# Layer 0's products in four 64x64 array tiles, with sums that stay in PSUM for a whole image

## The chip, the cores and the metric

The kernel runs on one core of one Trainium2 chip. The metric is the device time of one execution in microseconds (us). Five engines work side by side[...]: TensorE (PE in the profile, with PEld for its weight loads), VectorE (DVE), ScalarE (ACT), GpSimd (POOL) and SyncE (SP), which here only issues transfers. TensorE writes its results to PSUM, which has eight banks of 512 float32 values per partition; ScalarE and VectorE take them out from there.

## The reference, cut to what matters

Four layers follow each other on an input of 4 images with 64 x 64 = 4096 positions and 64 channels, all in float32. Layer 0 is the one that is changed:

```
q, k, v = x Wq + bq,  x Wk + bk,  x Wv + bv        # 4 images, 4096 x 64 each
attn    = softmax over keys of (q k^T)             # 4096 x 4096 per image
out[n]  = sum over queries m of attn[m, n] * v[m]  # summed over the queries, not over the keys
x       = gamma * out + x
```

Layer 1 is a block with two pointwise convolutions, a 3x3 depthwise convolution, a channel gate and two more pointwise convolutions. Layer 2 is an attention of the image with itself, and layer 3 an attention with 32 channels, followed by a normalisation over all images.

The unusual point of layer 0 is that `out` is summed over the queries. A query's row of `attn` can only be scaled once its whole sum of exponentials is known. That scale (one over the sum) goes into `v`, which gives a scaled row per query named `vq`. Then `out` is the product of `vq` with the plain exponentials, added up over all 4096 queries.

## The kernel before, in words

`fast_path` does the work; `general_path` is a second version that runs only if a check of the sums at the end of `fast_path` fails.

**Layout.** `X` holds image b as 128 partitions x 2048 columns: partitions 0 to 63 are the 64 channels of the first half of the positions, partitions 64 to 127 those of the second half. PSUM is split by two pools: `pp` has three tiles of two banks each (`new_ps`), and `pa` has two tiles of one bank each (`new_acc`).

**Layer 0, one tile of 128 queries** (`scores(t)`, t from 0 to 31). For each of four column groups g, four matmuls (line L1045) fill one `ps` tile of 128 queries x 1024 keys. Each works on 64 of the array's rows (64 channels) and 64 of its columns (64 queries), so that four of them together fill the array; I call four such matmuls a quad. A float32 matmul is two MATMUL records in the profile. ScalarE then takes the exponential of the whole `ps` tile into a tile `e` in SBUF (line L1050), and adds up its row sums on the way. `scale(t)` on VectorE turns the sums into `vq` (L1059, L1061, L1062).

**The products** (`products(p, half)`, L1070) take a pair of query tiles. Here the 128 queries are the contraction, so each matmul uses all 128 array rows and 64 columns, and two of them (one for each half of the keys) fill the array. A call runs two query tiles x two column groups x two key halves, that is 8 matmuls or four such pairs, into two `acc` banks. After each call VectorE adds the two banks, times gamma, into a running sum `m.y` in SBUF (`stt`, L1077).

**Order.** ScalarE, VectorE and TensorE run in the order in which the program is written. `run()` steps through a list `items`, one for every tile of queries; after each item the functions that fall due at it are called. For layer 0 an item is all four score quads of a tile in a row, and then comes one call of `products` (four pairs). Two generators fill in other work, the lanes `conv` and `misc`: `conv` runs layer 1 of the image before (`layer1`), `misc` loads, the projections of the next image (`project0`) and other preparations. A lane is ticked twice an item with the item's nominal cost (3.6), and makes a step when its own nominal time has come. The lanes take their PSUM from `new_ps` as the scores do.

**Layer 2**, which serves for comparison below, is built alike: `scores(n)` (L1259) are four quads of 64x64 and `products(n)` (L1276) are four quads of 64x64 too, since there the two query halves go to separate accumulators.

**Padding.** `layer1` takes a new padded buffer `pad` for each of its two halves and has GpSimd write its zero border (L1145 to L1147) each time.

Of the kernel before, what the change touches and what calls it, by code (L numbers as in the profile page):

```python
# [8 lines left out]
F32 = mybir.dt.float32  # L9
# [682 lines left out]
def fast_path(ctx: ExitStack, tc: tile.TileContext, a: dict, out: bass.AP, bad):  # L692
# [10 lines left out]
    tp = ctx.enter_context(tc.tile_pool(name="tp", bufs=2))  # L703
    xn = ctx.enter_context(tc.tile_pool(name="xn", bufs=1))
    sm = ctx.enter_context(tc.tile_pool(name="sm", bufs=2))
    pp = ctx.enter_context(tc.tile_pool(name="pp", bufs=3, space=PSUM))
    pa = ctx.enter_context(tc.tile_pool(name="pa", bufs=2, space=PSUM))

    PW = 65

    def new_ps(name="ps"):
        return pp.tile([128, 1024], F32, tag="ps", name=name)

    def new_acc(name="acc"):
        return pa.tile([128, 512], F32, tag="acc", name=name)

    def new_e(name="e"):
        return ep.tile([128, 2048], F32, tag="e", name=name)
# [4 lines left out]
    def new_big(name):  # L723
        return big.tile([128, 4096], F32, tag="big", name=name)
# [254 lines left out]

    def project0(b):  # L980
        x, m = X[:, b], im[b]
        m.q, yv = new_big("q"), new_big("yv")
        m.y = yv[:, 0:2048]
        m.v = yv[:, 2048:4096].rearrange("p (t c) -> p t c", c=C)
        once = ((0, "once"), (0, "v"), (1, "once"), (1, "v"))
        for j, w in once if b else ((0, "q"), (0, "v"), (1, "q"), (2, "q"), (1, "v"), (3, "q")):
            ps = new_ps()
            if w == "once":
                for o in range(2):
                    for s in range(2):  # L990
                        mm(
                            ps[64 * o : 64 * o + 64, bass.ts(s, 512)], wq[64 * s : 64 * s + 64, 0:64],
                            tok(x, s, 2 * j + o), start=True, stop=True,
                        )
                qs = m.q.rearrange("p (s n) -> p s n", s=2)
                for o in range(2):
                    own, other = slice(64 * o, 64 * o + 64), slice(64 - 64 * o, 128 - 64 * o)
                    n = bass.ts(2 * j + o, 512)
                    act(  # L999
                        qs[own, :, n], ps[own, :].rearrange("p (s n) -> p s n", s=2),  # L1000
                        AF.Identity, bias=bqk[own, :],
                    )
                    nc.sync.dma_start(out=qs[other, :, n], in_=qs[own, :, n])
            elif w == "q":
                for o in range(0, 128, 64):
                    for s in range(2):
                        mm(
                            ps[o : o + 64, bass.ts(s, 512)], wq[64 * s : 64 * s + 64, o : o + 64],
                            tok(x, s, j), start=True, stop=True,
                        )  # L1010
                for s in range(2):
                    nc.vector.tensor_scalar_add(
                        m.q[:, 2048 * s + 512 * j : 2048 * s + 512 * j + 512], ps[:, bass.ts(s, 512)], bqk
                    )
            else:
                for i in range(8):
                    mm(ps[:, bass.ts(i, 128)], x[:, bass.ts(8 * j + i, 128)], wv, start=True, stop=True)  # L1017
                for s in range(2):
                    nc.vector.tensor_add(
                        m.v[:, 16 * s + 8 * j : 16 * s + 8 * j + 8, :],  # L1020
                        ps.rearrange("p (t s c) -> p t s c", s=2, c=C)[:, :, s, :],
                        bv.unsqueeze(1).to_broadcast([128, 8, C]),
                    )
            yield 3.4

    between = []

    def layer0(b):  # L1030
        x, m, first = X[:, b], im[b], len(items)
        tiles = {}

        def scores(t):
            es = [new_e() for _ in range(2)]
            zs = sm.tile([128, 4], F32, tag="zs", name="zs", bufs=4)
            vq = sm.tile([128, C], F32, tag="vq", name="vq", bufs=4)
            for g in range(4):
                if g == 2 and between:
                    between.pop()()  # L1040
                ps = new_ps()
                for c in range(2):
                    for r in range(2):
                        rows_ = slice(64 * r, 64 * r + 64)
                        mm(  # L1045
                            ps[64 * c : 64 * c + 64, bass.ts(r, 512)],
                            m.q[rows_, 128 * t + 64 * c : 128 * t + 64 * c + 64],
                            x[rows_, bass.ts(g, 512)], start=True, stop=True,
                        )
                act(  # L1050
                    es[g // 2][:, bass.ts(g % 2, 1024)], ps, AF.Exp, bias=SHIFT0,
                    accum_out=zs[:, g : g + 1],
                )
            tiles[t] = es, vq, zs

        def scale(t):
            es, vq, zs = tiles[t]
            tot = sums0[:, b, t : t + 1]
            nc.vector.tensor_reduce(tot, zs, AX.X, ALU.add)  # L1059
            rec = sm.tile([128, 1], F32, tag="rec", name="rec")  # L1060
            nc.vector.reciprocal(rec, tot)  # L1061
            nc.vector.tensor_scalar_mul(vq, m.v[:, t, :], rec)  # L1062

        def products(p, half):
            accs = [new_acc() for _ in range(2)]
            for t in (2 * p, 2 * p + 1):
                es, vq, _ = tiles[t]
                for g in range(2):
                    for r in range(2):
                        mm(  # L1070
                            accs[g][64 * r : 64 * r + 64, :], vq,
                            es[half][:, 1024 * g + 512 * r : 1024 * g + 512 * r + 512],
                            start=t == 2 * p, stop=t == 2 * p + 1,
                        )
            for g in range(2):
                cols = bass.ts(2 * half + g, 512)
                stt(  # L1077
                    (x if p == 15 else m.y)[:, cols], accs[g], gam0,
                    (m.y if p else x)[:, cols], ALU.mult, ALU.add,
                )  # L1080

        for t in range(32):
            items.append((lambda t=t: scores(t), 3.6))
        for p in range(16):
            for half in range(2):
                at(first + 2 * p + 2 + half, lambda p=p, half=half: products(p, half))
        for t in range(32):
            at(first + t, lambda t=t: scale(t))


    def norm(x, y):
# [29 lines left out]
        for jp in range(2):  # L1121
            cols = bass.ts(jp, 1024)
            nc.vector.tensor_mul(y[:, cols], y[:, cols], x[:, cols])
            yield 1.8

    def layer1(b):
        x = X[:, b]

# [12 lines left out]
        yw = yg.rearrange("c (s q p h) -> c p q s h", s=2, p=2, h=H)  # L1141
        ysum = sm.tile([128, 8], F32, tag="ysum", name="ysum")
        for r in (1, 0):
            pad = new_pad()
            nc.gpsimd.memset(pad[:, 0:PW], 0.0)  # L1145
            nc.gpsimd.memset(pad[:, 65 * PW : 66 * PW + 2], 0.0)
            nc.gpsimd.memset(  # L1147
                pad[:, PW : 65 * PW].rearrange("p (w h) -> p w h", h=PW)[:, :, 0:1], 0.0
            )
            inner = pad[:, PW + 1 : 65 * PW + 1].rearrange("c (p q s h) -> c q p s h", p=2, s=2, h=PW)  # L1150
            for j in range(4):
                ps = new_ps()
# [92 lines left out]
    def layer2(b):  # L1245
# [7 lines left out]
        def scores(n):  # L1253
            ib = n // 8
            for jb in range(4 * (n % 8), 4 * (n % 8) + 4):
                ps = new_ps()
                for r, c in quads:
                    rows_ = slice(64 * r, 64 * r + 64)
                    mm(  # L1259
                        ps[64 * c : 64 * c + 64, bass.ts(r, 512)],  # L1260
                        m.ko[rows_, 128 * jb + 64 * c : 128 * jb + 64 * c + 64],
                        m.ko[rows_, bass.ts(2 * ib + r, 512)], start=True, stop=True,
                    )
                if jb % 2 == 0:
                    e = new_e()
                es[n, jb] = e[:, bass.ts(jb % 2, 1024)]
                act(es[n, jb], ps, AF.Exp, bias=SHIFT2, accum_out=m.zs[:, jb, ib : ib + 1])  # L1267

        def products(n):
            ib = n // 8  # L1270
# [94 lines left out]
    def layer3(b):  # L1365
# [23 lines left out]
        def products(n):  # L1389
# [3 lines left out]
                st["y"] = new_acc()  # L1393
            if mc % 10 == 9 or (last and n >= 60):
                if mc == 9:
                    st["z"] = new_acc("accz")
                for k in range(4):
                    mm(  # L1398
                        st["z"][32 * k : 32 * k + 32, :], ones[:, 0:32], e[:, bass.ts(k, 512)],
# [166 lines left out]

    def begin_out(i):
        b, g = i // 2, i % 2
        ps = new_ps("out")
        for k in range(8):  # L1570
            mm(
                ps[:, bass.ts(k, 128)], X[:, b, 1024 * g + 128 * k : 1024 * g + 128 * k + 128], ident,
                start=k % 4 == 0, stop=False,
            )
        return ps
# [125 lines left out]
        nc.vector.tensor_reduce(cnt, acc[0:1, 0:4], AX.X, ALU.add)  # L1701
        nc.vector.tensor_scalar(bad, cnt, -1.0, float(total), ALU.mult, ALU.add)

    with tc.manual_schedule(engines={mybir.EngineType.PE, mybir.EngineType.Activation, mybir.EngineType.DVE}):
        run()
        finish()

# [47 lines left out]
```

## Time and profile before

| | |
|---|---|
| time, median of 3 runs | 2637.28 us (2636.89 to 2637.54) |
| span of the profiled execution | 2635.8 us |
| TensorE busy | 2607.8 us, 99% |
| ScalarE busy | 1730.5 us, 66% |
| VectorE busy | 1331.1 us, 51% |
| GpSimd busy | 17.1 us, 1% |
| layer 0 (with the lanes' work in it) | about 17 to 1029 us of the span |

A busy TensorE is not a TensorE at its peak: matmuls overlap, their ends are modelled, and a wait inside the array counts as busy. The start of a group of matmuls in the timeline is exact, and so is the distance from one group's start to the next; that distance, and not the busy time, is what a group costs. PEld rows show when weights are loaded: in an undisturbed stream a weight load is done during the matmuls before it.

### The profile page before, as it was taken

The page shows a single profiled execution, that of the slowest core. Times are in us where ns is not written, and L with a number is a line of the kernel's source. Part 1 is how long each engine was busy: PE and PEld are TensorE (multiplying, and loading weights), DVE is VectorE, ACT ScalarE, POOL GpSimd, SP SyncE. Part 2 cuts the span into 40 slices and gives each one's busy share as a digit, 9 for nine tenths or more (in the row PEclk, how much of TensorE's full clock was granted, in tenths as well). Part 3 has the DMA queues.
Part 4 walks back from the last instruction along what each step waited for, and adds up shares of the span by engine and source line. Part 5 has one row for each costly group of instructions (what it writes and reads, how often), then busy time and mean ns, then how long its engine had stood idle before and what let it go on. Part 6 is the DMA issues. An engine that isn't in the chain of part 4 may idle for free.

```text
span 2635.8 us, 50835 instructions
## 1 busy us (share of the span) xinstructions
PE 2607.8 (99%) x22429; PEld 821.6 (31%) x22429; DVE 1331.1 (51%) x1542; ACT 1730.5 (66%) x2814; POOL 17.1 (1%) x67
## 2 busy tenths in 40 slices
PE   8999999999999999999999999999999999999998
PEld 3333233333323323333333322233322233322223
DVE  3232397633876338721772148800068600098997
ACT  4555656656565665666656678855678755578886
POOL 2000000000000000000000000000000000000000
PEclk9999999999999999999999999999999999999999
DMA  3000000001000100010010000010000010010002
GB/s 74 1 17 1 17 14 5 1 17 33 1 1 1 33 17 1 1 33 17 1 33 17 17 1 1 2 33 1 17 1 2 1 33 1 1 33 2 1 2 66
DMA packets 24538, 36.46 MB, mean 14 GB/s; under 512 B 3724, under 2 KB 12149, under 8 KB 24309
## 3 DMA queue, kind: packets, MB, share of 16 engines
q1 hardware_dynamic: 23285, 32.03, 5.5%
q8 instruction: 178, 2.92, 0.5%
q0 software_dynamic: 704, 0.56, 0.1%
q10 hardware_dynamic: 320, 0.54, 0.1%
q14 instruction: 51, 0.42, 0.1%
HBM read 4.80 MB, written 4.19 MB: 3 GB/s over the span
## 4 chain that ended last, share of the span: by engine, by line
PE 97%; ACT 1%; DVE 1%; issue 0%; DMA 0%; SPq 0%; ACTq 0%
PE acc L1070 17%; PE ps L1045 17%; PE acc L1276 17%; PE ps L1259 16%; PE ps L1377 11%; PE acc L1412 10%; PE ps L1132 2%; PE accz L1398 1%; PE ps L1017 1%; PE ps L1223 1%; PE ps L1200 1%; PE ps L1102 1%; PE ps L1356 1%; PE ps L931 0%; ACT e L1267 0%; PE ps L1289 0%
## 5 line engine op out<-in xcount | busy, mean ns | idle before, releaser
L1050 ACT ACTIVATE e<-ps 128x1024 f32<-128x1024 f32 x512 | 517.0, 1025 | 310.9 <-PE ps L1045 211.4
L1267 ACT ACTIVATE e<-ps 128x1024 f32<-128x1024 f32 x512 | 517.1, 1025 | 302.3 <-PE ps L1259 302.2
L1405 DVE TENSOR_TENSOR tg<-tg,e 128x2048 f32<-128x2048 f32 x213 | 488.1, 2292 | 24.0 <-ACT e L1383 5.7
L1045 PE MATMUL ps<-X,q 64*64 64x512 f32 x4096 | 474.5, 598 | 6.2 <-ACT q L999 1.7
L1259 PE MATMUL ps<-ko 64*64 64x512 f32 x4096 | 467.2, 591 | 2.2 <-ACT ko L1241 1.6
L1070 PE MATMUL acc<-e,vq 128*64 128x512 f32 x2048 | 467.4, 598 | 0.0
L1276 PE MATMUL acc<-e,X 64*64 64x512 f32 x4096 | 464.7, 591 | 0.3 <-DVE X L1077 0.3
L1077 DVE SCALAR_TENSOR_TENSOR yv<-acc,gam,yv 128x512 f32<-128x512 f32 x224 | 167.9, 750 | 324.8 <-PE acc L1070 314.0
L1382 ACT ACTIVATE e<-ps 128x1024 f32<-128x1024 f32 x256 | 262.8, 1027 | 84.4 <-PE ps L1377 70.3
L1171 DVE SCALAR_TENSOR_TENSOR y<-pad,vec,y 128x1024 f32<-128x1024 f32 x240 | 308.1, 1284 | 8.1 <-ACT pad L1155 1.0
L1377 PE MATMUL ps<-tg,ph 32*64 32x512 f32 x4096 | 311.0, 613 | 0.5 <-ACT e L1382 0.3
L1412 PE MATMUL acc<-e,tg 128*32 128x512 f32 x2048 | 271.8, 603 | 0.0
L1383 ACT ACTIVATE e<-ps 128x1024 f32<-128x1024 f32 x256 | 261.4, 1021 | 0.0
L1259 PEld LDWEIGHTS ps<-ko 64*64 64x64 f32 x4096 | 153.6, 132 | 292.0 <-issue 199.9
L1045 PEld LDWEIGHTS ps<-X,q 64*64 64x64 f32 x4096 | 143.0, 132 | 320.0 <-issue 222.1
L1276 PEld LDWEIGHTS acc<-e,X 64*64 64x64 f32 x4096 | 155.2, 133 | 277.1 <-issue 272.3
L1070 PEld LDWEIGHTS acc<-e,vq 128*64 128x64 f32 x2048 | 136.1, 136 | 314.6 <-issue 293.4
L1284 DVE TENSOR_TENSOR ph<-ph,acc 128x512 f32<-128x512 f32 x16 | 11.0, 688 | 392.2 <-ACT ph L1283 392.2
L1377 PEld LDWEIGHTS ps<-tg,ph 32*64 32x64 f32 x4096 | 80.5, 129 | 217.2 <-issue 119.7
L1267 ACT ACTIVATION_READ_ACCUMULATOR e<-ps 128x1 f32 x512 | 106.5, 208 | 0.0
L1412 PEld LDWEIGHTS acc<-e,tg 128*32 128x32 f32 x2048 | 43.6, 108 | 201.0 <-issue 196.9
L1050 ACT ACTIVATION_READ_ACCUMULATOR e<-ps 128x1 f32 x512 | 106.0, 207 | 0.0
(195 smaller groups left out, 981.5 us busy)
## 6 DMA issues: line engine op xcount, KB each, us to landing
xn<-t SPq DMA_DIRECT2D x64, 128.0 KB
ph<-tg SPq DMA_DIRECT2D x64, 128.0 KB
ko<-ko SPq DMA_DIRECT2D x16, 256.0 KB
xr<-in_x_dram SPq DMA_DIRECT2D x13, 256.0 KB
q<-q SPq DMA_DIRECT2D x12, 256.0 KB
out_dram<-o SPq DMA_DIRECT2D x8, 256.0 KB
out_dram<-o SPq DMA_DIRECT2D x4, 512.0 KB
xr<-in_x_dram ACTq DMA_DIRECT2D x2, 128.0 KB
```

What stands on the lines that cost most here:

```text
L1045: mm(ps[64 * c : 64 * c + 64, bass.ts(r, 512)], m.q[rows_, 128 * t + 64 * c : 128 * t + 64 * c + 64], x[rows_, bass.ts(g, 512)], start=Tru ...
L1050: act(es[g // 2][:, bass.ts(g % 2, 1024)], ps, AF.Exp, bias=SHIFT0, accum_out=zs[:, g : g + 1],)
L1070: mm(accs[g][64 * r : 64 * r + 64, :], vq, es[half][:, 1024 * g + 512 * r : 1024 * g + 512 * r + 512], start=t == 2 * p, stop=t == 2 * p + 1,)
L1171: stt(y1, win, wt, y1, ALU.mult, ALU.add)
L1259: mm(ps[64 * c : 64 * c + 64, bass.ts(r, 512)], m.ko[rows_, 128 * jb + 64 * c : 128 * jb + 64 * c + 64], m.ko[rows_, bass.ts(2 * ib + r, 5 ...
L1267: act(es[n, jb], ps, AF.Exp, bias=SHIFT2, accum_out=m.zs[:, jb, ib : ib + 1])
L1276: mm(acc[r][64 * c : 64 * c + 64, :], xw[rows_, jb, :], es[n, jb][rows_, bass.ts(c, 512)], start=jb == 0, stop=jb == 31,)
L1377: mm(tiles[kp][64 * c : 64 * c + 64, bass.ts(i, 512)], m.ph[rows_, 128 * mc + 64 * c : 128 * mc + 64 * c + 64], m.th[rows_, bass.ts(nb, 51 ...
L1382: act(e[:, 0:1024], tiles[0], AF.Exp)
L1383: held.append(lambda: act(e[:, 1024:2048], tiles[1], AF.Exp))
L1405: nc.vector.tensor_add(esum, esum, e)
L1412: mm(st["y"][32 * k : 32 * k + 32, :], m.gx[:, i % 32, :], es[i][:, bass.ts(k, 512)], start=mc == 0, stop=i % 32 == 31,)
```

## The change

**The products** (`product(t, i)`) are cut into four calls for each tile of queries, and each is a quad of 64x64 matmuls. The 128 queries are split into two row halves r. In one quad, row half 0 adds to the bank of column group i and row half 1 to the bank of group i + 2 (modulo 4), each for both key halves s. After four calls both halves have been added to all four banks. The sums stay there for all 32 tiles of an image, so that the additions into `m.y` go away; at the last tile VectorE adds the four banks into `X`.

**PSUM.** The two pools become one tile `PS` with all eight banks. Banks 4 to 7 hold the sums during layer 0, so that only two score slots are left there (`take_slots(0, 1)`) instead of three. After layer 0 the slots are the three of before and `new_acc` has banks 6 and 7.

**Row halves.** The two row halves of the array write the same bank in alternate calls. To keep them apart, the first matmul of a product waits until the product two calls earlier has ended. It waits for an empty instruction on GpSimd (`nop`), which itself waits for the last matmul of that earlier product.

**Order.** Within an item a score quad and a product quad alternate: score (t, g), a tick of each lane (1.8), for g = 0 the `scale` of the tile before, then the product that is six calls behind (`LAG`). The products that are left at the end of an image run among the next image's scores, or after each score quad of layer 2's first image (`follow(0)`).

**Padding.** The padded buffer is one for the whole kernel, and its border is written once.

```diff
-    pp = ctx.enter_context(tc.tile_pool(name="pp", bufs=3, space=PSUM))
-    pa = ctx.enter_context(tc.tile_pool(name="pa", bufs=2, space=PSUM))
+    pp = ctx.enter_context(tc.tile_pool(name="pp", bufs=1, space=PSUM))
...
+    PS = pp.tile([128, 4096], F32, name="PS")
+    turn_of = {"slots": [0, 1, 2, 3], "ps": 0, "acc": 0}
+
+    def new_ps():
+        s = turn_of["slots"][turn_of["ps"] % len(turn_of["slots"])]
+        turn_of["ps"] += 1
+        return PS[:, bass.ts(s, 1024)]
...
-        def products(p, half):
-            accs = [new_acc() for _ in range(2)]
-            for t in (2 * p, 2 * p + 1):
-                es, vq, _ = tiles[t]
-                for g in range(2):
-                    for r in range(2):
-                        mm(
-                            accs[g][64 * r : 64 * r + 64, :], vq,
-                            es[half][:, 1024 * g + 512 * r : 1024 * g + 512 * r + 512],
-                            start=t == 2 * p, stop=t == 2 * p + 1,
-                        )
-            for g in range(2):
-                cols = bass.ts(2 * half + g, 512)
-                stt(
-                    (x if p == 15 else m.y)[:, cols], accs[g], gam0,
-                    (m.y if p else x)[:, cols], ALU.mult, ALU.add,
-                )
+        def product(t, i):
+            if b == 0 and t == 0 and i == 0:
+                take_slots(0, 1)
+            es, vq, _ = tiles[t]
+            for s in range(2):
+                for r in range(2):
+                    j, rows_ = (i + 2 * r) % 4, slice(64 * r, 64 * r + 64)
+                    k = 1024 * (j % 2) + 512 * s
+                    ins = mm(
+                        PS[64 * s : 64 * s + 64, 2048 + 512 * j : 2560 + 512 * j], vq[rows_, :],
+                        es[j // 2][rows_, k : k + 512],
+                        start=t == 0 and i < 2, stop=t == 31 and i >= 2,
+                    ).ins
+                    if s == r == 0 and len(steps) > 1:
+                        wait_for(ins, steps[-2])
+            steps.append(nc.gpsimd.nop(nofuse=True).ins)
+            wait_for(steps[-1], ins)
+            if t == 31 and i >= 2:
+                for j in (i, i - 2) if b == B - 1 else (i - 2, i):
+                    xs = x[:, bass.ts(j, 512)]
+                    stt(xs, PS[:, 2048 + 512 * j : 2560 + 512 * j], gam0, xs, ALU.mult, ALU.add)
+                if b == B - 1 and i == 3:
+                    take_slots(0, 1, 2)
...
+            for g in range(4):
+                if g == 2 and between:
+                    between.pop()()
+                score(t, g)
+                late.append(lambda g=g: product(t, g))
+                for lane in (conv, misc):
+                    lane.tick(1.8)
+                if g == 0 and t:
+                    scale(t - 1)
+                follow()
...
-            pad = new_pad()
-            nc.gpsimd.memset(pad[:, 0:PW], 0.0)
```

## The prediction

> **What bounds the kernel now.** I read the page's table of busy times first, then the list of lines, then the timeline of one undisturbed stretch of layer 0 beside one of layer 2.
>
> ```profile
> span 2635.8 us, 50835 instructions
> PE 2607.8 (99%) x22429; PEld 821.6 (31%) x22429; DVE 1331.1 (51%) x1542; ACT 1730.5 (66%) x2814; POOL 17.1 (1%) x67
> ...
> L1045 PE MATMUL ps<-X,q 64*64 64x512 f32 x4096 | 474.5, 598 | 6.2 <-ACT q L999 1.7
> L1259 PE MATMUL ps<-ko 64*64 64x512 f32 x4096 | 467.2, 591 | 2.2 <-ACT ko L1241 1.6
> L1070 PE MATMUL acc<-e,vq 128*64 128x512 f32 x2048 | 467.4, 598 | 0.0
> L1276 PE MATMUL acc<-e,X 64*64 64x512 f32 x4096 | 464.7, 591 | 0.3 <-DVE X L1077 0.3
> ```
>
> TensorE has no idle time to speak of, so the span is the sum of what its groups cost; another engine can only matter by making TensorE wait. The four lines are the scores and products of layers 0 and 2. By busy time they are nearly alike, and the change seems worth nothing: 512 quads take the place of 512 pairs. But busy time counts overlap twice, so I turn to the starts. Layer 0, TensorE alone:
>
> ```profile
> 202.15 3.66 PE L1045 MATMUL ps<-X,q 64*64 64x512 f32 x32
> 205.74 3.65 PE L1070 MATMUL acc<-e,vq 128*64 128x512 f32 x16
> 209.32 3.66 PE L1045 MATMUL ps<-X,q 64*64 64x512 f32 x32
> 212.92 3.65 PE L1070 MATMUL acc<-e,vq 128*64 128x512 f32 x16
> ```
>
> and layer 2:
>
> ```profile
> 1278.22 3.61 PE L1276 MATMUL acc<-e,X 64*64 64x512 f32 x32
> 1281.65 3.61 PE L1259 MATMUL ps<-ko 64*64 64x512 f32 x32
> 1285.09 3.61 PE L1276 MATMUL acc<-e,X 64*64 64x512 f32 x32
> 1288.52 3.61 PE L1259 MATMUL ps<-ko 64*64 64x512 f32 x32
> ```
>
> From start to start, four score quads and four product pairs of layer 0 take 212.92 - 205.74 = 7.18 us. In layer 2 eight quads take 1288.52 - 1281.65 = 6.87 us, for the same number of multiplications. The 0.31 us between them lies at the two places where layer 0 changes the array's shape. The weight loads show it:
>
> ```profile
> 208.37 0.14 PEld L1070 LDWEIGHTS acc<-e,vq 128*64 128x64 f32 x2 [0.28 <-issue]
> 209.32 0.21 PEld L1045 LDWEIGHTS ps<-X,q 64*64 64x64 f32 x8 [0.81 <-issue]
> 209.81 0.15 PEld L1045 LDWEIGHTS ps<-X,q 64*64 64x64 f32 x4 [0.28 <-issue]
> 210.24 0.15 PEld L1045 LDWEIGHTS ps<-X,q 64*64 64x64 f32 x4 [0.28 <-issue]
> ```
>
> Within a shape a load comes every 0.43 us (0.15 busy, 0.28 idle), half a quad ahead of its matmuls. Before the first load of another shape there are 0.81 us of idle time, and that load starts together with its matmuls instead of ahead of them.
>
> **What the Trainium skill says.** "TensorEngine Tiling (Array Packing)", section Key Properties: "Changing tiling mode (not just tile) drains the TensorE". The trace agrees, and sets the size: 0.31 us for two switches, so 0.156 us for one. The same page, section "Gotcha 1: PSUM Pressure", says that different row tiles may not be in one bank at the same time and that software has to see to it. That is what the new wait is for; nothing in the trace of before shows the case. "TensorE: Matmul & The Clock Gate", Part 3, section "The mechanism", says that weight loads are pulled ahead of running matmuls; the 0.43 us rhythm agrees.
>
> **The change part by part.**
>
> *Switches removed.* The order of TensorE's instructions in the two programs tells where the array's shape differs from one matmul to the next. From the first to the last matmul of layer 0 there are 291 switches before and 91 after; outside layer 0 it is 628 and 627. The 91 are the lanes' matmuls of other shapes, which now always lie between two 64x64 quads. So 200 x 0.156 = 31.1 us go.
>
> *Rate of the new quads.* 512 quads for 512 pairs. Layer 2's L1276 is a product with exactly this shape: 3.43 us for four, 0.858 each. A pair in the middle of L1070 has the same rhythm (0.43 us for each half). Alternating single quads instead of runs of four should cost nothing: in layer 2 a single lane quad (L1132) between scores and products takes 0.86 to 0.91 us. Change: 0.
>
> *The new wait.* Each product waits for the empty GpSimd instruction of the product two calls earlier. Between that product's end and the waiting one lie two score quads and one product, 3 x 0.858 = 2.57 us. The trace has no such round trip. Nearest row: an exponential of layer 0 that ended at 204.32 released a weight load at 204.47, 0.15 us later. Two such hops and the empty instruction give 0.3 to 0.5 us by my estimate, and even 1 us would be hidden behind the 2.57. Behind the waiting matmul stands all of TensorE, but it waits for nothing that is late. GpSimd has nothing else to do by then: its last border write starts at 16.58 us and the first product before starts at 33.70 us. The 127 products that wait for VectorE as well (`vq`) may need a separate sequencer instruction, 51 ns each by the rows of L1045; 6.5 us if none is hidden, 0 if the sequencer is ahead as in the rest of the stream. I take 0 and keep 6.5 for the range.
>
> *Two score slots instead of three.* A slot is taken again two scores later. From a score's end to the start of the score that needs its slot lie product, score, product: 2.57 us. ScalarE needs about 0.25 to start (the quad that began at 202.15 was through at about 203.06, the exponential began at 203.30), 1.02 for the exponential and 0.15 to release: 1.42. With 4 x 1.0 us in 6.87 it keeps up. When a lane step comes between, it takes a slot: then only the lane quad and a product lie between, 1.72 us against 1.42. That still holds, but the weight load, which wants to go 0.43 us ahead, may be late: about 0.05 us, what a switch shows at its entry. The order shows 88 lane steps in layer 0. Those with long ScalarE work (the two squares of `norm`, 2 x 1.03; the 2 x 1.03 of `project0`) or a VectorE evacuation behind a depthwise tap (1.28) overrun by a few tenths. I put the sum at 88 x 0.05 + 20 x 0.3 = 10 us at most in addition. Against it stands what three slots cost now: in runs of four scores the fourth waits for the first one's exponential, and next to a lane step TensorE really loses time (a score group of 3.78 us instead of 3.43 at 1250.82). By my sum over all groups of layer 0, 12.3 us are such losses, 4.5 of them in the first 35 us. Single scores between products do not run into this. New minus old: +2 us, between -8 and +10.
>
> *Additions removed.* 256 of L1077 at 0.75 us become 16: 180 us of VectorE. VectorE is not the bound, but where the depthwise taps run it needs 4 x 1.28 + 2 x 0.75 + 0.57 = 7.2 us an item, just what the item lasts, and ScalarE then waits for taps at the border between the two halves of `layer1`. That gets easier, and is in the -8. The last additions of an image: two of 0.75 us must be done before the next image's first product, which is 2.57 us later; hidden unless a tap stands ahead. 1 us for three borders, inside the +2.
>
> *Padding, lag of six, order of the lanes.* Border writes by GpSimd were not on the path. The exponential's tiles are six; with a lag of six products the oldest pair is free one score before it is needed. Nominal lane time is 7.2 an item before and after, so the lanes stay in step. 0.
>
> Sum: 2637.3 - 31.1 + 2 = 2608 us.
>
> **The rivals.**
>
> *Two slots starve the scores.* For: a lane step has only 0.3 us of slack, and two lanes at once have none. Against: at most 88 places. With 0.1 to 0.3 us at each, 9 to 26 us come back: 2615 to 2632, middle 2622.
>
> *The new rhythm exposes every weight load, or the wait through GpSimd is never early enough.* Then each of 1024 quads loses 0.05 us, the part of a switch that shows when the load is not ahead: 51 - 31 = 20 us slower, 2657. If the round trip took 3 us instead of 0.5, 512 products would lose 0.4 us each and it would be 2810. For: no such wait is in the trace. Against: scores already wait for ScalarE one by one, and where this is satisfied in time the 0.43 us rhythm has no dent.
>
> *More than the switches.* If the losses of 12.3 us shrink to the 4.5 of the start: 2637.3 - 31.1 - 7.8 = 2598.
>
> *No change.* A gain of 31 us that is just cancelled: 2632 to 2643.
>
> **How the numbers follow.** Forecast (2603 to 2614): 0.62. Starved slots: 0.17. More than the switches: 0.12. Slower: 0.06. No change: 0.03. The range takes the forecast, most of "more", and the nearer half of the starved slots: 2597 to 2624. Faster: 0.62 + 0.17 + 0.12 = 0.91; same 0.03; slower 0.06.
>
> **What would show it.** Right: in an undisturbed item of layer 0 eight quads take 6.87 us from start to start, and the weight loads keep 0.43 us through score and product alike, with 0.81 us only beside lane steps of other shapes. The slots are right if the scores' idle time on ScalarE's account stays under 10 us in sum. Wrong: weight loads of the products that wait for GpSimd, or score groups next to lane steps that begin several tenths late.

## The result, and the profile after

The changed kernel takes 2604.08 us (median of 4 runs, 2603.85 to 2604.50) where the kernel before takes 2637.09 us (2636.84 to 2637.54). The ratio is 0.9875, with a 95% interval of 0.9858 to 0.9892: 33.0 us less. The forecast was 2608 us, in a range of 2597 to 2624.

The page of the changed kernel, busy times and the groups of layers 0 and 2 (L1058 and L1084 are layer 0's scores and products, L1289 and L1307 layer 2's):

```profile
span 2602.6 us, 55344 instructions
PE 2571.1 (99%) x24477; PEld 870.6 (33%) x24477; DVE 1163.0 (45%) x1302; ACT 1770.1 (68%) x2814; POOL 14.3 (1%) x46
...
L1084 PE MATMUL PS<-e,vq 64*64 64x512 f32 x4096 | 540.0, 591 | 0.0
L1058 PE MATMUL PS<-X,q 64*64 64x512 f32 x4096 | 536.4, 590 | 1.8 <-DVE X L942 1.7
...
L1289 PE MATMUL PS<-ko 64*64 64x512 f32 x4096 | 469.2, 591 | 2.2 <-ACT ko L1271 1.7
L1307 PE MATMUL PS<-e,X 64*64 64x512 f32 x4096 | 464.1, 591 | 0.0
```

Here the busy time misleads. Layer 0's two groups seem to have grown from 942 to 1076 us. They have not: with single quads in turn, the overlap of each quad with the next is now counted in both groups. The starts tell the cost. TensorE of the changed kernel in an undisturbed stretch of layer 0:

```profile
206.00 1.04 PE L1058 MATMUL PS<-X,q 64*64 64x512 f32 x8
206.86 1.04 PE L1084 MATMUL PS<-e,vq 64*64 64x512 f32 x8
207.72 1.04 PE L1058 MATMUL PS<-X,q 64*64 64x512 f32 x8
208.58 1.04 PE L1084 MATMUL PS<-e,vq 64*64 64x512 f32 x8
209.44 1.04 PE L1058 MATMUL PS<-X,q 64*64 64x512 f32 x8
```

Each quad is "busy" for 1.04 us, but the next starts after 0.86. Four quads take 209.44 - 206.00 = 3.44 us, so eight take about 6.87 (from the trace, 206.00 to 212.87), where four quads and four pairs took 7.18 before. The weight loads of the same stretch:

```profile
206.00 0.15 PEld L1058 LDWEIGHTS PS<-X,q 64*64 64x64 f32 x4 [0.28 <-issue]
206.43 0.15 PEld L1084 LDWEIGHTS PS<-e,vq 64*64 64x64 f32 x4 [0.28 <-POOLq L1091]
206.86 0.15 PEld L1084 LDWEIGHTS PS<-e,vq 64*64 64x64 f32 x4 [0.28 <-issue]
207.29 0.15 PEld L1058 LDWEIGHTS PS<-X,q 64*64 64x64 f32 x4 [0.28 <-issue]
```

The 0.43 us rhythm runs through scores and products alike, and the idle stretch of 0.81 us at each change of shape is gone. The product's load names GpSimd's empty instruction as its releaser, but comes no later for it.

Added up from start to start over the whole trace, scores and products of layer 0 went from 469.0 and 458.0 us to 452.9 and 442.7: 31.4 us less. The pointwise quads of layer 1, which now have their own shape on both sides, give 2.7 more. Another 2.8 are one wait for `norm`'s squares in layer 2. It goes with the order and not with the shape: it is there in the kernel before and in the two experiments below with scores in runs of four, and it is gone in the one with the old shape in the new order. In all the last matmul starts at 2591.84 us instead of 2628.28, that is 36.4 us earlier. 3.3 us of this are lost after it (last section), which leaves the span's 33.2.

### The profile page after: what moved, and what is told of

Its sections match the earlier page's. It is cut to its first block, busy times and chain, and to the rows that moved or that the text cites. A ratio compares the mean times of both kernels' runs of the same rounds, so it can differ in the third digit from the quotient of the medians.

```text
span 2602.6 us, 55344 instructions
## 1 busy us (share of the span) xinstructions
PE 2571.1 (99%) x24477; PEld 870.6 (33%) x24477; DVE 1163.0 (45%) x1302; ACT 1770.1 (68%) x2814; POOL 14.3 (1%) x46
## 4 chain that ended last, share of the span: by engine, by line
PE 96%; ACT 2%; DVE 1%; DMA 0%; issue 0%; SPq 0%; ACTq 0%; DVEq 0%
PE PS L1307 17%; PE PS L1289 17%; PE PS L1084 16%; PE PS L1058 16%; PE PS L1408 11%; PE PS L1443 10%; PE PS L1168 2%; PE PS L1429 1%; ACT e L1063 1%; PE PS L1026 1%; PE PS L1230 1%; PE PS L1253 1%; PE PS L1133 1%; PE PS L1387 1%; ACT q L1008 0%; PE PS L941 0%
## 5 line engine op out<-in xcount | busy, mean ns | idle before, releaser
L1063 ACT ACTIVATE e<-PS 128x1024 f32<-128x1024 f32 x512 | 524.2, 1024 | 325.5 <-PE PS L1058 283.1
L1297 ACT ACTIVATE e<-PS 128x1024 f32<-128x1024 f32 x512 | 517.2, 1025 | 292.3 <-PE PS L1289 289.1
L1084 PE MATMUL PS<-e,vq 64*64 64x512 f32 x4096 | 540.0, 591 | 0.0
L1058 PE MATMUL PS<-X,q 64*64 64x512 f32 x4096 | 536.4, 590 | 1.8 <-DVE X L942 1.7
L1289 PE MATMUL PS<-ko 64*64 64x512 f32 x4096 | 469.2, 591 | 2.2 <-ACT ko L1271 1.7
L1307 PE MATMUL PS<-e,X 64*64 64x512 f32 x4096 | 464.1, 591 | 0.0
L1413 ACT ACTIVATE e<-PS 128x1024 f32<-128x1024 f32 x256 | 262.8, 1027 | 84.5 <-PE PS L1408 63.6
L1408 PE MATMUL PS<-tg,ph 32*64 32x512 f32 x4096 | 311.1, 613 | 0.5 <-ACT e L1413 0.5
L1443 PE MATMUL PS<-e,tg 128*32 128x512 f32 x2048 | 271.8, 603 | 0.0
L1414 ACT ACTIVATE e<-PS 128x1024 f32<-128x1024 f32 x256 | 261.3, 1021 | 0.0
L1058 PEld LDWEIGHTS PS<-X,q 64*64 64x64 f32 x4096 | 161.4, 133 | 279.2 <-issue 231.8
L1289 PEld LDWEIGHTS PS<-ko 64*64 64x64 f32 x4096 | 156.6, 132 | 290.0 <-issue 199.7
L1084 PEld LDWEIGHTS PS<-e,vq 64*64 64x64 f32 x4096 | 160.9, 133 | 272.7 <-issue 170.9
L1307 PEld LDWEIGHTS PS<-e,X 64*64 64x64 f32 x4096 | 155.5, 133 | 275.0 <-issue 271.5
L1297 ACT ACTIVATION_READ_ACCUMULATOR e<-PS 128x1 f32 x512 | 106.5, 208 | 0.0
L1063 ACT ACTIVATION_READ_ACCUMULATOR e<-PS 128x1 f32 x512 | 99.6, 195 | 0.1
```

The lines of the kernel that those rows point to most:

```text
L1058: mm(ps[64 * c : 64 * c + 64, bass.ts(r, 512)], m.q[rows_, 128 * t + 64 * c : 128 * t + 64 * c + 64], x[rows_, bass.ts(g, 512)], start=Tru ...
L1063: act(es[g // 2][:, bass.ts(g % 2, 1024)], ps, AF.Exp, bias=SHIFT0, accum_out=zs[:, g : g + 1],)
L1084: ins = mm(PS[64 * s : 64 * s + 64, 2048 + 512 * j : 2560 + 512 * j], vq[rows_, :], es[j // 2][rows_, k : k + 512], start=t == 0 and i < 2 ...
L1289: mm(ps[64 * c : 64 * c + 64, bass.ts(r, 512)], m.ko[rows_, 128 * jb + 64 * c : 128 * jb + 64 * c + 64], m.ko[rows_, bass.ts(2 * ib + r, 5 ...
L1307: mm(acc[r][64 * c : 64 * c + 64, :], xw[rows_, jb, :], es[n, jb][rows_, bass.ts(c, 512)], start=jb == 0, stop=jb == 31,)
L1408: mm(tiles[kp][64 * c : 64 * c + 64, bass.ts(i, 512)], m.ph[rows_, 128 * mc + 64 * c : 128 * mc + 64 * c + 64], m.th[rows_, bass.ts(nb, 51 ...
```

## The experiments

**The shape alone undone.** Products as 128x64 pairs again, everything else as in the changed kernel; the wait through GpSimd goes too, since pairs have no row halves to keep apart. This and the next two experiments were run once each.

```diff
-            for s in range(2):
-                for r in range(2):
-                    j, rows_ = (i + 2 * r) % 4, slice(64 * r, 64 * r + 64)
-                    k = 1024 * (j % 2) + 512 * s
...
+            for s in range(2):
+                k = 1024 * (i % 2) + 512 * s
+                mm(
+                    PS[64 * s : 64 * s + 64, 2048 + 512 * i : 2560 + 512 * i], vq,
+                    es[i // 2][:, k : k + 512], start=t == 0, stop=t == 31,
+                )
...
```

> The changed kernel with only the array's shape undone: products as 128x64 pairs again (two matmuls over all 128 queries, one for each key half), straight into the four banks, so no wait through GpSimd is needed; order, slots, lag, padding and removed additions stay. By the order of TensorE's instructions the shape changes 1054 times in layer 0 instead of 91. Theory (drains at a change of shape, 0.156 us each): 963 x 0.156 = 150 us more than the changed kernel's 2604, about 2754 us. Rival (the gain came from the order, from the sums in PSUM or from VectorE's relief): no slower than 2604 to 2610.

Measured: 2752.23 us, 148.2 above the changed kernel. From the first score to the last product this trace has 1054 changes of shape and the changed kernel's 85, so it is 0.153 us for each of 969. (The 91 of the forecast takes in six changes ahead of the first score, hence its 963.) TensorE in this run:

```profile
205.64 1.08 PE L1082 MATMUL PS<-e,vq 128*64 128x512 f32 x4
206.65 1.09 PE L1058 MATMUL PS<-X,q 64*64 64x512 f32 x8
207.67 1.08 PE L1082 MATMUL PS<-e,vq 128*64 128x512 f32 x4
```

Start to start is now 1.01 to 1.02 us instead of 0.86, at every step of this stretch. Order, sums in PSUM and VectorE's relief are all still there, and without the shape the kernel is 115 us slower than before the change, because the finer order changes the shape nearly four times as often (1054 to 285). So these three alone don't bring the gain, and a change of shape costs what was forecast.

**The alternation alone undone.** Four score quads, then four product quads, all 64x64, with two slots.

```diff
                 score(t, g)
                 late.append(lambda g=g: product(t, g))
-                for lane in (conv, misc):
-                    lane.tick(1.8)
-                if g == 0 and t:
-                    scale(t - 1)
-                follow()
+            for lane in (conv, misc):
+                lane.tick(3.6)
+            if t:
+                scale(t - 1)
+            for g in range(4):
+                follow()
+            for lane in (conv, misc):
+                lane.tick(3.6)
```

> The changed kernel with only the alternation undone: four score quads in a row, then four product quads, all 64x64, two slots as in the changed kernel. 81 changes of shape in layer 0. Theory: the shape is what saves time, but two slots bear only scores that alternate with products: in a run the third score waits for the first exponential (0.56 us) and the fourth for the second (0.16 us), 0.72 us or more an item, 92 us in all, 2696 us; up to 2725 if a product that follows its neighbour at once also waits for GpSimd. Rival (order is of no account): 2604.

Measured: 2741.39 us, more than the estimate's upper end. An undisturbed item:

```profile
206.83 1.90 PE L1058 MATMUL PS<-X,q 64*64 64x512 f32 x16
209.16 2.10 PE L1058 MATMUL PS<-X,q 64*64 64x512 f32 x16 [0.44 <-ACT e L1063]
211.08 3.61 PE L1084 MATMUL PS<-e,vq 64*64 64x512 f32 x32
214.51 1.04 PE L1058 MATMUL PS<-X,q 64*64 64x512 f32 x8
```

The third score begins 2.33 us after the first instead of 1.72, waiting for the exponential that frees its slot; the item takes 7.68 us, 0.81 more than 6.87, or 104 us over 128 items. The four products take 3.43 us, so a product right behind its neighbour does not wait for GpSimd. Of the other 33 us, the sums from start to start put about 15 in the scores, 12 in the products, 3 in the wait for `norm`'s squares in layer 2 and the rest in the lanes. In the scores they lie beside lane groups: the 47 whole runs of four with such a group before or behind them take 1.40 us more than four times 0.858, the 77 without take 0.79 more. That a lane group does this by taking one of the two slots is argued and not shown by itself. With three slots scores in a row take 3.43 us in an undisturbed stretch (next run), so what needs the alternation is the two slots, not the shape.

**The shape alone changed in the kernel before**, with its two accumulator banks (and the border of the padded buffer written once).

```diff
+            for q in range(2):
+                for t in (2 * p, 2 * p + 1):
...
+                            g, rows_ = (q + r) % 2, slice(64 * r, 64 * r + 64)
...
+                            if q == 1 and t == 2 * p and s == r == 0:
+                                wait_for(ins, step)
+                if q == 0:
+                    step = nc.gpsimd.nop(nofuse=True).ins
+                    wait_for(step, ins)
```

> The kernel before with only the products' shape changed: 64x64 quads into its two accumulator banks, four score quads and then four product quads, additions into the running sum kept; with two banks the row halves must change banks in the middle of a call, and the first quad after that waits (through an empty GpSimd instruction) for the quad just before it. Borders of the padded buffer written once, so that nothing stands ahead of that instruction. Changes of shape in layer 0: 81 instead of 291, worth 33 us. Theory: TensorE stands still at each of 128 such waits for the round trip, estimated at 0.5 to 0.7 us with the lost lead of the weights: 2637 - 33 + 64 to 90, about 2668 to 2694. Rival (the round trip costs nothing): 2604.

Measured: 2660.22 us, somewhat below the estimate. TensorE and its weight loads around one call of products:

```profile
200.85 3.98 PE L1077 MATMUL acc<-e,vq 64*64 64x512 f32 x32
204.66 3.61 PE L1049 MATMUL ps<-X,q 64*64 64x512 f32 x32
208.09 1.47 PE L1077 MATMUL acc<-e,vq 64*64 64x512 f32 x12
```

```profile
201.71 0.15 PEld L1077 LDWEIGHTS acc<-e,vq 64*64 64x64 f32 x4 [0.28 <-issue]
202.89 0.21 PEld L1077 LDWEIGHTS acc<-e,vq 64*64 64x64 f32 x8 [1.02 <-POOLq L1084]
203.37 0.15 PEld L1077 LDWEIGHTS acc<-e,vq 64*64 64x64 f32 x4 [0.28 <-issue]
```

The scores take 3.43 us, the products 3.81: the bare wait costs 0.38 us a call, 49 us in all, which is more than the 32 us that 204 fewer changes of shape bring. The 6 us that are still missing to the measured time are 4 us of further losses in the scores and 2 at the end of the program. So the shape pays only if other work lies between the two row halves' turns on a bank. Four banks give this even where products follow each other: a bank passes to the other half two calls later, and in the undisturbed item of the previous experiment, with four products in a row, none waits. The next experiment shows that one score in between is enough, so the new order would give it too; two banks in the new order were not tried.

**A tighter wait in the changed kernel**: for the product just before (one score quad of slack) instead of the one two calls earlier.

```diff
-                    if s == r == 0 and len(steps) > 1:
-                        wait_for(ins, steps[-2])
+                    if s == r == 0 and len(steps) > 0:
+                        wait_for(ins, steps[-1])
```

> The changed kernel with a tighter wait: each product waits for the end of the product just before it instead of the one two calls earlier. Between the two lies one score quad, 0.86 us, instead of 2.57. Theory: the round trip through GpSimd takes 0.3 to 0.5 us and the weights want to go 0.43 us ahead, so this is at the edge: 0 to 0.07 us for each of 512 products, 2604 to 2640 us, likeliest 2612. If the round trip were 1 us or more: over 2604 + 512 x 0.5 = 2860. If it were quite hidden: 2604.

Measured: 2603.60 us (2602.73 to 2604.83), ratio 0.9870 (0.9854 to 0.9887): no difference from the changed kernel. Its loads keep the rhythm with the product's released by GpSimd:

```profile
206.67 0.15 PEld L1058 LDWEIGHTS PS<-X,q 64*64 64x64 f32 x4 [0.28 <-issue]
207.10 0.15 PEld L1084 LDWEIGHTS PS<-e,vq 64*64 64x64 f32 x4 [0.28 <-POOLq L1091]
```

My estimate of the round trip, 0.3 to 0.5 us, was too long; 0.86 us hides round trip and lead of the weights together.

**VectorE's load put back**: two additions an item, used nowhere.

```diff
...
                 follow()
+                if g % 2:
+                    cols = bass.ts((2 * t + g // 2) % 4, 512)
+                    stt(m.y[:, cols], x[:, cols], gam0, x[:, cols], ALU.mult, ALU.add)
```

> The changed kernel with VectorE's load put back: two additions of 128x512 an item into an unused half of the buffer of v, from X instead of from PSUM (about 0.7 us each, some 180 us of VectorE in all); their result is used nowhere. Theory (VectorE was not the bound and its relief is worth little): 2604 to 2608 us. Rival (much of the gain is VectorE's relief): 2610 to 2635.

Measured: 2606.37 us (2604.91 to 2607.83), ratio 0.9880 (0.9864 to 0.9897). So the relief of VectorE is worth at most about 2 us of the 33; the slowest run of the changed kernel (2605.16 us, in the last series below) reaches into this range.

**The padded buffer as before**, with GpSimd writing its border each time.

```diff
...
         for r in (1, 0):
+            pad = new_pad()
+            nc.gpsimd.memset(pad[:, 0:PW], 0.0)
...
```

> The changed kernel with the padded buffer as before: taken anew for each half of layer 1, its border written by GpSimd each time, so that the empty instructions which products wait for stand behind a border write that waits for VectorE's last tap. Theory (VectorE is ahead of its place, the writes take some 0.5 us and the wait has 2.57 us of slack): 2604 to 2607 us. Rival (the writes hold up TensorE): each of 7 rewritten buffers costs 1 to 3 us, 2611 to 2625.

Measured: 2603.28 us (2602.23 to 2604.12), ratio 0.9870 (0.9854 to 0.9887): nothing. The empty instructions stand behind those border writes, but come in time.

**Can the rest be had?** Two slots leave losses beside some lane steps. In the changed kernel's trace, TensorE and then ScalarE beside `norm`:

```profile
268.66 1.04 PE L1084 MATMUL PS<-e,vq 64*64 64x512 f32 x8
269.52 1.04 PE L1058 MATMUL PS<-X,q 64*64 64x512 f32 x8
271.39 1.07 PE L1133 MATMUL PS<-X,jsel 128*32 128x512 f32 x8 [0.84 <-ACT e L1063]
```

```profile
267.24 1.02 ACT L1063 ACTIVATE e<-PS 128x1024 f32<-128x1024 f32 x1 [0.65 <-ACT e L1063]
268.16 0.20 ACT L1063 ACTIVATION_READ_ACCUMULATOR e<-PS 128x1 f32 x1
268.25 1.99 ACT L1127 ACTIVATE sq<-X 128x1024 f32<-128x1024 f32 x2
270.15 1.01 ACT L1063 ACTIVATE e<-PS 128x1024 f32<-128x1024 f32 x1
```

Two squares in a row hold ScalarE for 2 us; the exponential behind them begins at 270.15, although TensorE had left its scores (the quad before 268.66) more than a microsecond earlier, and the matmuls that want its slot stand still until 271.39, 0.84 us. Two tries follow. The first eases two steps: the squares of `norm`, and the two instructions with which `project0` takes its results out of PSUM (the evacuations).

```diff
         for i in range(2):
             act(sq[i], x[:, bass.ts(i, 1024)], AF.Square)
-        yield 4.0
+            yield 2.0
...
+                    if o:
+                        nc.vector.tensor_scalar_add(qs[own, :, n], src, bqk[own, :])
+                    else:
+                        act(qs[own, :, n], src, AF.Identity, bias=bqk[own, :])
```

> The changed kernel with two steps eased that leave TensorE waiting for a slot in its trace: the two squares of norm (2 x 1.0 us of ScalarE) become two lane steps, and of the two evacuations of project0 (2 x 1.1 us of ScalarE) one goes to VectorE. In the changed kernel's trace the groups beside these steps lose about 9 us. Theory (what is left of layer 0's losses is ScalarE late at these steps, with only two slots to buffer it): 2596 to 2600 us. Rival (the losses only move, or VectorE's evacuation stands behind taps): 2603 to 2608.

Measured: 2602.27 us (2601.41 to 2603.12), ratio 0.9866 (0.9849 to 0.9882), short of the estimate. Beside `norm` the losses went away. At `project0` they stayed: VectorE's part began only when ScalarE's on the same slot had ended.

```profile
636.46 1.29 DVE L1010 TENSOR_SCALAR q<-PS,bqk 64x1024 f32<-64x1024 f32 x1 [5.38 <-ACT q L1012]
```

The slot was held as long as before. So the second try leaves the evacuations alone and moves them to a time when layer 1 needs no slot:

```diff
-            misc_from[32 * b + 16] = gens + [project0(b + 1)]
+            misc_from[32 * b + (22 if b else 16)] = gens + [project0(b + 1)]
```

> The changed kernel with the two squares of norm as two lane steps (as in the run smooth, where the losses beside norm went away), both evacuations of project0 on ScalarE as in the changed kernel, and project0 of images 2 and 3 started six items later (22 instead of 16 items into layer 0), when layer 1 runs its taps and takes no PSUM slot. Theory (a slot is missing only where two lanes take one within two scores): of the losses of 10 us in the changed kernel's layer 0 about half go, 2598.5 to 2601 us. Rival (they come back behind VectorE's taps): 2602 to 2605.

> The changed kernel itself, once more on the chip of the run before it, to compare with: 2603.5 to 2604.5 us by every theory.

Measured, on the same chip: 2600.55 us (2598.77 to 2600.85), ratio 0.9859 (0.9843 to 0.9876), and the changed kernel again 2604.36 us (2604.22 to 2605.16), ratio 0.9876 (0.9859 to 0.9892). The runs of the two don't overlap, and this version beats both kernels by its medians, the changed one by 3.8 us. TensorE beside the same `norm`:

```profile
269.39 1.04 PE L1084 MATMUL PS<-e,vq 64*64 64x512 f32 x8
270.25 1.04 PE L1058 MATMUL PS<-X,q 64*64 64x512 f32 x8
271.21 1.07 PE L1133 MATMUL PS<-X,jsel 128*32 128x512 f32 x8
```

0.96 us instead of 1.87 from the score to `norm`'s matmuls, and no wait. Of the nine steps in layer 0 that lose 0.7 to 1.0 us in the changed kernel's trace, three are left in this one.

## Why the prediction was right

*Switches removed.* Right in kind and size. 200 fewer changes of shape at 0.156 us were forecast to bring 31.1 us. From the first score to the last product the traces have 285 changes before and 85 after, which is the forecast 200. Scores and products fell by 31.4 us, of which I count about 29 to the switches and 2 to smaller waits (below); with the 2.7 us of the pointwise quads the switches come to about 32. The run with 969 more gives 0.153 each.

*Rate of the new quads.* Right: 0.858 us, as read from layer 2, and single quads in turn cost nothing.

*The new wait.* Right that it is hidden; the round trip was put too long (0.3 to 0.5 us, against 0.14 in the last section). The 128 sequencer instructions for products with two waits (51 ns each) are in the trace, and the rhythm has no dent from them.

*Two score slots.* The term was +2 us, as a balance of old losses gone and new ones come; it came out at about -2. I take as loss what scores and products of layer 0 take from start to start beyond 0.858 us a quad and 0.156 us a change of shape. It was 12.7 us before and is 10.5 after. In the first 35 us it fell from 3.6 to 0.7: the first product starts at 25.37 us instead of 33.70 and fills waits there. After that it rose from 9.1 to 9.8. (If the lanes' groups are counted too, by what each loses against the fastest of its like, the sum hardly falls, from 13.5 to 13.3 us; so the balance is known to some 2 us.) The old losses in runs of scores went away, and new ones came at steps with long ScalarE work. There the forecast had the kind right and the parts wrong: it counted 88 places at 0.05 us and 20 at 0.3, and the trace has nine with 0.7 to 1.0 us, 7.6 in sum, and little elsewhere. That the sum still fits the forecast's 10 us at most is luck. The scores' own loss, 9.1 us, is just under the 10 that were named as the limit. The rival of starved slots held for these nine steps alone. It would have been right for scores in runs, as the second experiment shows.

*Additions and padding.* Right: at most about 2 us, and nothing.

*What the sum missed.* By TensorE's last matmul the gain is 36.4 us instead of the forecast 29. Of the 7 us between them about 4 are the balance of the slots (-2 instead of +2), and 2.8 are the wait for `norm`'s squares in layer 2, which was not in my sum. At the end of the program 3.3 us were lost, which was not in it either. These errors go opposite ways, and the 4 us by which the forecast missed are what is left of them; that it came so near is partly luck. The rival "more than the switches" was closer to the gain at the last matmul, but not for its reason: the losses of the start shrank, and the others did not.

## What to carry to other kernels

When TensorE is full, compare the distance from start to start of like groups in two stages, not their busy times: here busy times differed by 1% and later pointed the wrong way, while the starts showed 0.31 us an item. Array shapes that alternate cost time at every change (0.15 us here, in float32 with 512 columns), so count the changes in the order of the instructions and multiply. A new shape may need a wait of its own (two row halves on one bank), and whether it pays is decided by the order and the banks that hide this wait: the same quads gained 33 us with four banks in the new order and lost 23 with two banks in the old one.

## What the runs showed of the hardware

The way through GpSimd is short. In the run with the bare wait, the last matmul before it ended at 202.75 us by the modelled end, GpSimd's instruction ran at 202.82 for 17 ns, and TensorE's load started at 202.89: 0.14 us there and back, and much the same at all 128 such waits. In the changed kernel these instructions read:

```profile
L1091 POOLq EVENT_SEMAPHORE  x512: 17/17/17, 27.1 to 1006.4; - x171
```

The bare wait costs more, 0.38 us. An estimate from the same traces accounts for it: a quad of an undisturbed stream is busy for 1.04 us by its modelled end and the next starts after 0.86, so 0.18 us of overlap are lost when the next has to wait for that end. With the 0.14 us of the round trip and 0.05 for a first load that no longer runs ahead (202.89 to 203.37 instead of 0.43) this makes 0.37.

The end of the program is not constant. From the start of the last matmul to the end of the span it takes 7.5 us in the trace of before, 10.8 in the changed kernel's, and 8.9 with the padding of before; the other versions lie between 9.6 and 11.1. The same kinds of instruction stand there (loading the flag, the branch over `general_path`, the final semaphores). In the kernel before, GpSimd is through its semaphores behind the branch 2.2 us after the last matmul started, and 2.5 us of closing work run beside SyncE's waits. In the changed kernel it stands at the third of them until 7.1 us, the time at which SyncE's wait ends too, and the closing work comes behind. No run was made to find out why; this stays open.
